# Start of the expert tiles, scaling of their results and the final additions in an attention + mixture-of-experts kernel

## The chip, the cores and the metric

The kernel runs on one core of a Trainium2 chip. The metric is the device time of one execution in microseconds; before the change its median was 694.02 us over three runs (693.63 to 695.32). The engines are TensorE (PE; its weight loads PEld), VectorE (DVE), ScalarE (ACT), GpSimd (POOL) and SyncE (SP), which here only issues transfers.

## The reference, cut to what matters

The input x has 64 batch rows of 128 tokens with 128 features, all fp32. A gated cross-attention with 16 heads (context of 77 tokens) comes first, then a gated mixture of 8 experts:

```python
x = x + tanh(g_xattn[0]) * xattn(layernorm(x), ctx_768, ...)
n = layernorm(x)
gate_scores = softmax(n @ Wg)                       # 8 experts
topk_scores, topk_idx = top_k(gate_scores, 2)
topk_scores = topk_scores / (topk_scores.sum(-1) + 1e-08)
gate  = einsum('bsh,ehi->bsei', n, W11)             # i = 256
value = einsum('bsh,ehi->bsei', n, W12)
fused = gate * sigmoid(gate) * value
expert_out = einsum('bsei,eih->bseh', fused, W2)
x = x + tanh(g_ffn[0]) * sum over the two picked experts of topk_scores * expert_out
```

The kernel computes only the two picked experts of each token: 64 x 128 x 2 = 16,384 token rows.

## The kernel before

**Attention.** The 64 batch rows are handled in 16 groups of 4 (NG, G). A loop over i = 0 to 65 (L970 to L991) does, for one batch row at a time, scores, turning of the probabilities (`turn`) and the product with the values (`mix`, L914). Everything else of a group (loads, layernorm, keys, gate, places, dispatches) is a list of named steps. A planner's table says at which i, and whether before or after the main work of that i (PRE or POST), each step is due (AT, TURN, EARLY, SCHED); `advance(i, where)` runs those that are due. Instructions keep, on each engine, the order in which the program emits them, and each engine works through its own in order.

**From tokens to tiles.** For each group, DVE picks the two experts, POOL counts them (`counts`, L685 to L694), TensorE turns counts into places and DVE into row numbers (`places_in`, `dest` L717). Then POOL writes every token row to its expert's region in DRAM: `dispatch` (L719 to L730) is a memset of a spare buffer of 128x320 (L721), which keeps two indirect transfers apart in time, and an indirect DMA (L722). There are eight to a group, one for each batch row b and choice k (`dispatch{b}{k}`), 128 in all. The groups form two parts: groups 0 to 11 (SPLIT = 12) fill 103 tiles of 128 rows, groups 12 to 15 fill 39. When a part is full, `tiles_count` to `tiles_keep` (L753 to L820) work out which rows and which expert each tile has.

**Tiles.** After the attention loop its pools are closed and those of the tiles are opened in the space that comes free. One step of the tile loop is `tile_steps(t)` (L1081 to L1084), which works on tiles of different age:

- `load` (L1013 to L1021), tile t: SP fetches the tile's rows xt (pool lp, 26 buffers)
- `turned` (L1023), tile t: TensorE transposes (ptt, L1025), DVE copies to xTt (L1027)
- `up` (L1029), tile t-2: two up products pu (L1035), ACT's silu (sgt, L1041), DVE's product (ht, L1043)
- `flip` (L1047), tile t-4: two transposes phh (L1050), ACT's copy to hTt (L1052)
- `down` (L1054), tile t-6: four products pot (L1058), DVE scales by the token's gate weight into y (L1064), then POOL does its memset (L1065) and scatters the rows of y to the result buffer yb in DRAM (L1066)

**Beside the tiles.** The steps of groups 12 to 15 that the attention loop leaves over are in the list `rest` (L1109) and are run a few at each tile, their dispatches included, so POOL does 32 dispatches among its scatters. Results come back by group: `fetch` (L1089, SP) reads both results of each token (ys), `combine` (L1099) adds them to xs with two DVE additions of 128x512 (L1101), `store` (L1103) sends the sum out by ACT's queue. For groups 0 to 11 the table `at` sets the step: fetch of group g at t0 + 2g with t0 = 122, combine three steps and store six steps later. Groups 12 to 15 follow after the tile loop, all fetches first. A fetch waits until all scatters of its part have landed.

Of the kernel before, what the change touches and what calls it, by code (L numbers as in the profile page):

```python
# [8 lines left out]
F32 = mybir.dt.float32  # L9
# [3 lines left out]
AF = mybir.ActivationFunctionType  # L13
ALU = mybir.AluOpType
AX = mybir.AxisListType
PSUM = bass.MemoryType.PSUM
# [5 lines left out]
G = 4  # L22
# [2 lines left out]
JL = 16  # L25
PRE, POST = 0, 1
TOPK = 2
RW = 132
APART = 320
PAST = 1 << 20  # L30
# [2 lines left out]
SPLIT = 12  # L33
# [3 lines left out]
def tile_gated_xattn_moe(  # L37
# [17 lines left out]
    nc = tc.nc  # L55
    B, S, D = x.shape
    M, CD = context.shape[1:]
    E, _, I = W11.shape
    P = 128
    NG = B // G  # L60
# [3 lines left out]
    scale = HD**-0.5  # L64
    NTOK = B * S
    class Part:


        def __init__(self, c, g0, g1):
# [24 lines left out]
    xs = [keep.tile([P, G, D], F32, tag=f"x{g}", name=f"x{g}") for g in range(NG)]  # L94
# [99 lines left out]

    empty = const.tile([P, RW], F32, name="empty")
    nc.gpsimd.memset(empty[:, :D], 0.0)
    nc.gpsimd.iota(empty[:, D:].bitcast(I32), [[0, RW - D]], base=PAST, channel_multiplier=0)
    tg = const.tile([P, 2], F32, name="tg")
# [17 lines left out]
    for q in range(NQ):  # L216
        for k in range(2):
            r = 32 * q + 16 * k
            nc.sync.dma_start(
                out=wo_in[r : r + 16], in_=Wo[32 * q + 16 * (1 - k) : 32 * q + 16 * (2 - k)]  # L220
# [74 lines left out]
    spare_w = const.tile([P, APART], F32, name="spare_w")  # L295
# [12 lines left out]
    with ExitStack() as ph:  # L308
        s2 = ph.enter_context(tc.tile_pool(name="s2", bufs=2))
        s3 = ph.enter_context(tc.tile_pool(name="s3", bufs=3))  # L310
        s4 = ph.enter_context(tc.tile_pool(name="s4", bufs=4))
        s5 = ph.enter_context(tc.tile_pool(name="s5", bufs=5))
        ph.enter_context(tc.manual_schedule(engines={PE, ACT, DVE, POOL}))

        nc.scalar.activation(tg, gates, AF.Tanh)
# [14 lines left out]
        def apart(i, group):  # L330

            i = getattr(i, "ins", i)
            tc.declare_no_dep(i, group=group, reason="rows of their own")
            tc.add_to_no_dep_group(group, i)
# [45 lines left out]
        ring = [ps_r]  # L380
# [4 lines left out]
        def transposed(src, n):  # L385
# [12 lines left out]
        AT = {  # L398
            "loads": (-15, PRE),
            "stats_a0": (-14, PRE),  # L400
            "sel_0": (-14, PRE),
            "stats_a1": (-10, PRE),
            "sel_1": (-13, PRE),
            "shift_a": (-9, POST),
            "sel_2": (-11, POST),
            "context_t": (-7, POST),
# [42 lines left out]
        TURN = {}  # L449
# [157 lines left out]
        def rows_f0(gr, g):  # L607
            pt = part_of(g)
            gr.rows = s5.tile([P, G, TOPK, RW], F32, tag="rows", name=f"rows_{g}")
            gr.xn = gr.rows[:, :, 0, :D]  # L610
            for k in range(TOPK):
                nc.gpsimd.iota(
                    gr.rows[:, :, k, D:].bitcast(I32), [[TOPK, G], [0, RW - D]],
                    base=TOPK * G * (g - pt.g0) + k, channel_multiplier=TOPK * pt.nb,
# [289 lines left out]
        def mix(b, va, pT, gr, n):  # L904
# [23 lines left out]
        NBT = NG * G  # L928
# [16 lines left out]
        EARLY = {  # L945
            (n, 1): 2 * i + where
            for n, i, where in (
                ("rows_a0", 1, PRE), ("rows_a1", 1, PRE), ("context_t", 1, POST),
                ("queries_t", 1, POST), ("queries", 2, POST), ("keys", 2, POST),
            )  # L950
        }
        EARLY["rows_a0", 2], EARLY["rows_a1", 2] = 4, 5
        EARLY["context_t", 2], EARLY["queries_t", 2], EARLY["queries", 2] = 6, 6, 7
        SCHED = {}
        for h in range(2 * min(TURN)[0], 2 * (NBT + 3)):
            for g in range(NG):
                for n in TURN.get((h // 2 - G * g, h % 2), ()):
                    if (n, g) not in FIRST:
                        SCHED.setdefault(EARLY.get((n, g), max(h, 1)), []).append((n, g))

        def run(steps):
            for n, g in steps:
                STEP[n](groups[g], g)

        def advance(i, where):
            run(SCHED.get(2 * i + where, ()))

        pes, vas, pTs = {}, {}, {}
        run(FIRST)
        for i in range(NBT + 2):  # L970
# [10 lines left out]
            if 0 <= i - 2 < NBT:  # L981
                g, b = divmod(i - 2, G)
# [5 lines left out]
                turn_last(pTs[i - 1], i - 1)  # L988
            advance(i, POST)
        advance(NBT + 2, PRE)  # L990
        advance(NBT + 2, POST)  # L991
        at_.close()
        after[0] = True


        lp = ph.enter_context(tc.tile_pool(name="lp", bufs=26))
        yp = ph.enter_context(tc.tile_pool(name="yp", bufs=20))
        hp = ph.enter_context(tc.tile_pool(name="hp", bufs=4))
        cb = ph.enter_context(tc.tile_pool(name="cb", bufs=4))
        ps_u = ph.enter_context(tc.tile_pool(name="ps_u", bufs=2, space=PSUM))  # L1000
        ps_t = ph.enter_context(tc.tile_pool(name="ps_t", bufs=1, space=PSUM))
        ring[0] = ph.enter_context(tc.tile_pool(name="ps_q", bufs=2, space=PSUM))

        wxf = wx.rearrange("p e i -> p (e i)")
        known = "built on the chip from counts, never past the last tile or expert"
# [7 lines left out]
        def load(ti, t):  # L1013
            pt = ti.pt
            r = nc.values_load(
                pt.tab[0:1, 0, ti.k : ti.k + 1], engines=(SP,), min_val=0,
                max_val=E * pt.cap + (pt.spare - 1) * P,
                skip_runtime_bounds_check_because=known,
            )
            ti.x = lp.tile([P, RW], F32, tag="x", name=f"xt_{t}")  # L1020
            nc.sync.dma_start(out=ti.x, in_=pt.xg[bass.ds(r, P), :])  # L1021

        def turned(ti, t):  # L1023
# [28 lines left out]
            nc.scalar.copy(ti.hT, pt)  # L1052

        def down(ti, t):  # L1054
            po = ps_u.tile([P, D], F32, tag="pd", name=f"pot_{t}")
            for c in range(NC):
                w = 2 * I + c * D
                nc.tensor.matmul(  # L1058
                    po, ti.hT[:, c],
                    wxf[:, bass.ds(ti.e + w, D)],  # L1060
                    start=(c == 0), stop=(c == NC - 1),
                )
            y = yp.tile([P, D], F32, tag="y", name=f"y_{t}")
            nc.vector.tensor_scalar_mul(y, po, ti.x[:, D + 1 : D + 2])  # L1064
            nc.gpsimd.memset(spare_w, 0.0)  # L1065
            i = nc.gpsimd.indirect_dma_start(  # L1066
                out=ti.pt.yb[:, :],
                out_offset=bass.IndirectOffsetOnAxis(
                    ap=ti.x[:, D : D + 1].bitcast(I32), axis=0
                ),  # L1070
                in_=y,
                in_offset=None,
                bounds_check=TOPK * ti.pt.ntok - 1,
                oob_is_err=False,
            )
            apart(i, f"results{ti.pt.c}")


        ts = [Tile(pt, k) for pt in parts for k in range(pt.nt)]

        def tile_steps(t):  # L1081
            for lag, f in ((0, load), (0, turned), (2, up), (4, flip), (6, down)):
                if 0 <= t - lag < len(ts):
                    f(ts[t - lag], t - lag)  # L1084


        ys = {}

        def fetch(g):  # L1089
            pt = part_of(g)  # L1090
            ys[g] = cb.tile([P, G, TOPK, D], F32, tag="ys", name=f"ys_{g}")
            i = TOPK * G * (g - pt.g0)
            nc.sync.dma_start(
                out=ys[g].rearrange("p b k d -> p (b k d)"),
                in_=pt.yb.rearrange("(t i) d -> t i d", t=S)[:, i : i + TOPK * G]
                .rearrange("t i d -> t (i d)"),
            )

        def combine(g):  # L1099
            for k in range(TOPK):  # L1100
                nc.vector.tensor_tensor(xs[g], xs[g], ys[g][:, :, k], ALU.add)  # L1101

        def store(g):  # L1103
            nc.scalar.dma_start(
                out=out[G * g : G * g + G].rearrange("b t d -> t b d"), in_=xs[g]
            )


        rest = [  # L1109
            (f, g)  # L1110
            for i in range(NBT + 3, G * (NG - 1) + max(TURN)[0] + 1)
            for where in (PRE, POST)
            for g in range(NG)
            for f in TURN.get((i - G * g, where), ())
        ]
        at = {}
        t0 = parts[0].nt + 19
        for g in range(SPLIT):
            for k, f in enumerate((fetch, combine, store)):
                at.setdefault(t0 + 2 * g + 3 * k, []).append((f, g))  # L1120
        t = 0
        while t < len(ts) + 6 or rest or any(k >= t for k in at):
            tile_steps(t)
# [2 lines left out]
            for f, g in at.get(t, ()):  # L1126
                f(g)
            t += 1
        for g in range(SPLIT, NG):
            fetch(g)  # L1130
        for g in range(SPLIT, NG):
            combine(g)
            store(g)

# [31 lines left out]
```

## Time and profile before

| | us |
|---|---|
| median of three runs | 694.02 |
| the profiled execution, its own time | 692.33 |
| its span on the core | 690.2 |
| PE busy | 615.3 (89%) |
| DVE busy | 466.1 (68%) |
| POOL busy | 442.0 (64%) |
| ACT busy | 392.9 (57%) |

Busy time is an average over stages of different kind: the attention stage runs to about 380 us, the tile stage from there to about 677, and the last four groups' results to 690.2. The profile has a line for each group of instructions (line of the kernel, engine, operation, output<-input and shape, count, busy time, mean of one in ns, and the idle time before it with what ended it). In a timeline a row is a start time, a duration, the engine and the instruction; the brackets at its end hold the engine's idle time before it and what ended that. "issue" is idle time in which the engine waited for nothing that the profile shows.

### The profile page before, as it was taken

The page shows a single profiled execution, that of the slowest core. Times are in us where ns is not written, and L with a number is a line of the kernel's source. Part 1 is how long each engine was busy: PE and PEld are TensorE (multiplying, and loading weights), DVE is VectorE, ACT ScalarE, POOL GpSimd, SP SyncE. Part 2 cuts the span into 40 slices and gives each one's busy share as a digit, 9 for nine tenths or more (in the row PEclk, how much of TensorE's full clock was granted, in tenths as well). Part 3 has the DMA queues.
Part 4 walks back from the last instruction along what each step waited for, and adds up shares of the span by engine and source line. Part 5 has one row for each costly group of instructions (what it writes and reads, how often), then busy time and mean ns, then how long its engine had stood idle before and what let it go on. Part 6 is the DMA issues. An engine that isn't in the chain of part 4 may idle for free.

```text
span 690.2 us, 21369 instructions
## 1 busy us (share of the span) xinstructions
PE 615.3 (89%) x7703; PEld 429.2 (62%) x7703; DVE 466.1 (68%) x1440; ACT 392.9 (57%) x1042; POOL 442.0 (64%) x769
## 2 busy tenths in 40 slices
PE   4799999999999999999988699999978999999770
PEld 3577777776776677676666266666555665656450
DVE  4758798788878887887797356465455454546673
ACT  3697888787877787787655433543432333333220
POOL 4411125577557755765565488888888888887671
PEclk9999999999999999999999899999999999999995
DMA  4493001111110100000110342222222313264666
GB/s 105 124 280 94 16 15 29 38 32 39 33 40 31 32 27 26 26 31 22 34 57 22 84 106 73 75 71 71 80 79 68 103 59 90 80 204 124 194 187 205
DMA packets 64510, 53.55 MB, mean 78 GB/s; under 512 B 14131, under 2 KB 58235, under 8 KB 64408
## 3 DMA queue, kind: packets, MB, share of 16 engines
q1 hardware_dynamic: 46424, 30.52, 16.5%
q0 software_dynamic: 8640, 17.06, 7.5%
q10 hardware_dynamic: 9344, 4.62, 2.4%
q8 instruction: 63, 1.03, 0.6%
q14 instruction: 39, 0.32, 0.2%
HBM read 28.88 MB, written 24.20 MB: 77 GB/s over the span
## 4 chain that ended last, share of the span: by engine, by line
PE 71%; DVE 9%; ACT 6%; issue 5%; POOL 5%; DMA 3%; another core or an unknown queue 1%; POOLq 0%; ACTq 0%; DVEq 0%; SPq 0%
PE pu L1035 16%; PE po L914 11%; PE tp L882 8%; PE pot L1058 7%; PE sc L860 5%; PE phh L1050 4%; PE ptt L1025 3%; PE tl L895 3%; POOL yb L1066 3%; PE pq L561 3%; PE py L584 2%; PE pc L523 2%; PE pg L637 2%; PE pv L833 2%; DVE x L1101 2%
## 5 line engine op out<-in xcount | busy, mean ns | idle before, releaser
L722 POOL DMA_INDIRECT xg<-rows,dest x128 | 127.1, 993 | 66.3 <-DVE gm L644 41.9
L1066 POOL DMA_INDIRECT yb<-y,xt x142 | 140.8, 992 | 41.4 <-issue 13.3
L1035 PE MATMUL pu<-wx,xTt 128*128 x284 | 153.7, 623 | 8.5 <-issue 7.6
L1041 ACT ACTIVATE sgt<-pu 128x256 f32<-128x256 f32 x142 | 54.5, 384 | 170.3 <-PE pu L1035 97.9
L1043 DVE TENSOR_TENSOR ht<-sgt,pu 128x256 f32<-128x256 f32 x142 | 59.6, 420 | 98.9 <-ACT sgt L1041 59.4
L869 DVE TENSOR_REDUCE mx<-sc 128x16 f32<-128x1232 f32 x64 | 91.6, 1431 | 22.4 <-PE sc L860 21.2
L1050 PEld LDWEIGHTS phh<-ident,ht 128*128 128x128 f32 x284 | 39.4, 141 | 79.6 <-issue 68.3
L1058 PE MATMUL pot<-wx,hTt 128*128 x568 | 87.0, 276 | 0.3 <-issue 0.3
L887 ACT ACTIVATE pT<-tp,drop 128x512 f32<-128x512 f32 x128 | 80.3, 677 | 9.9 <-PE tp L882 9.9
L872 DVE TENSOR_TENSOR pe<-sc,mx 128x1024 f32<-128x1024 f32 x64 | 78.4, 1224 | 2.2
L1058 PEld LDWEIGHTS pot<-wx,hTt 128*128 128x128 f32 x568 | 75.0, 192 | 0.4 <-issue 0.4
L914 PE MATMUL po<-pT,own 128*32 128x128 f32 x1536 | 66.9, 274 | 8.1 <-issue 7.8
L882 PEld LDWEIGHTS tp<-ident,pe 128*128 128x128 f32 x512 | 55.6, 142 | 27.9 <-issue 8.9
L882 PE MATMUL tp<-ident,pe 128*128 128x128 f32 x512 | 70.8, 282 | 0.9 <-ACT kb L550 0.6
L914 PE MATMUL po<-pT,va 128*32 128x128 f32 x1536 | 60.8, 274 | 2.3 <-issue 2.0
L1064 DVE TENSOR_SCALAR y<-pot,xt 128x128 f32<-128x128 f32 x142 | 49.0, 347 | 19.9 <-PE ptt L1025 8.5
L1052 ACT COPY hTt<-phh 128x256 f32<-128x256 f32 x142 | 52.3, 368 | 9.8 <-PE ptt L1025 5.5
L1050 PE MATMUL phh<-ident,ht 128*128 128x128 f32 x284 | 54.8, 275 | 3.1 <-ACT hTt L1052 1.9
L914 PEld LDWEIGHTS po<-pT,own 128*32 128x32 f32 x1536 | 46.2, 110 | 17.3 <-issue 17.1
L860 PE MATMUL sc<-kb,qT 32*128 32x308 f32 x512 | 52.5, 480 | 4.4 <-DVE pls L872 2.6
L365 POOL TENSOR_TENSOR rs_a<-rs_a,live 128x4 f32<-128x4 f32 x15 | 3.0, 199 | 81.9 <-ACT rs_a L362 74.1
L1035 PEld LDWEIGHTS pu<-wx,xTt 128*128 128x128 f32 x284 | 43.4, 193 | 19.0 <-issue 17.5
(167 smaller groups left out, 1109.9 us busy)
## 6 DMA issues: line engine op xcount, KB each, us to landing
xt<-xg SPq DMA_DIRECT2D x142, 66.0 KB
ys<-yb SPq DMA_DIRECT2D x16, 512.0 KB
out_dram<-x ACTq DMA_DIRECT2D x16, 256.0 KB
x<-in_x_dram SPq DMA_DIRECT2D x15, 256.0 KB
yb<-y,xt POOLq DMA_INDIRECT x142
wx<-in_L_ffn_W_dram SPq DMA_DIRECT2D x2, 1024.0 KB
xg<-rows,dest POOLq DMA_INDIRECT x128
xg<-empty SPq DMA_DIRECT2D x30, 66.0 KB
```

The lines of the kernel that those rows point to most:

```text
L722: i = nc.gpsimd.indirect_dma_start(out=part_of(g).xg[:, :], out_offset=bass.IndirectOffsetOnAxis(ap=gr.dest[:, k, b : b + 1], axis=0), in_ ...
L860: nc.tensor.matmul(sc[:, q, :W], gr.qT[r, b * S : (b + 1) * S], gr.kb[r, b].rearrange("p h j -> p (h j)"), start=True, stop=True,)
L869: nc.vector.tensor_reduce(mx[:, :, :, 0], sv, AX.X, ALU.max)
L872: nc.vector.tensor_tensor(dst[:, :, :, : j1 - j0], sv[:, :, :, j0:j1], mx.to_broadcast([P, NQ, HQ, j1 - j0]), ALU.subtract,)
L882: nc.tensor.transpose(tp[:, u, :], pe[:, q + u // 2, 2 * (u % 2) : 2 * (u % 2) + 2].rearrange("p h j -> p (h j)"), ident,)
L887: nc.scalar.activation(pT[:, 2 * q : 2 * q + 4], tp, AF.Exp, bias=drop[:, 0, i : i + 1], scale=scale)
L914: nc.tensor.matmul(po[32 * q : 32 * q + 32, v, :], w, pT[:, 2 * q + c if c < 2 else 8 + q // 2, :], start=(c == 0), stop=(c == 2),)
L1035: nc.tensor.matmul(pu.rearrange("p j i -> p (j i)"), ti.xT, wxf[:, bass.ds(ti.e, 2 * I)], start=True, stop=True,)
L1043: nc.vector.tensor_tensor(ti.h.rearrange("p c i -> p (c i)"), sg, pu[:, 1], ALU.mult)
L1050: nc.tensor.transpose(pt[:, c], ti.h[:, c], ident)
L1058: nc.tensor.matmul(po, ti.hT[:, c], wxf[:, bass.ds(ti.e + w, D)], start=(c == 0), stop=(c == NC - 1),)
L1066: i = nc.gpsimd.indirect_dma_start(out=ti.pt.yb[:, :], out_offset=bass.IndirectOffsetOnAxis(ap=ti.x[:, D : D + 1].bitcast(I32), axis=0), i ...
```

## The change

Six edits:

1. A pool l0 with 8 buffers (NL0) is opened beside attention's pools; the rows of the first 8 tiles are loaded into it, the others into lp as before. The pool hp (xT, sg, h, hT) is opened there too. The pools in PSUM are opened in another order, and pot has a pool of its own, ps_d.
2. The dispatches of batch rows 2 and 3 of group 11 are brought forward to the place of 18 after the group's first row, POST. The steps of (NBT + 2, POST), before run ahead of the tiles, become the first of `rest`.
3. y is made by ScalarE (a Copy with the gate weight as its scale) instead of DVE's multiplication.
4. For the last four tiles, POOL's memset covers one column instead of 320.
5. `combine` does one addition. For groups 0 to 11 fetches begin at step 112 (before 122), one each 28/12 steps, and the 24 additions are spread over steps 115 to 141, about one at each; the store goes with the second.
6. Of the last groups, fetched and added in the order 12, 15, 13, 14, group 15's two additions are done by POOL and its store is issued on SP's queue.

```diff
+NL0 = 8
...
+        l0 = ph.enter_context(tc.tile_pool(name="l0", bufs=NL0))
+        hp = ph.enter_context(tc.tile_pool(name="hp", bufs=4))
         ph.enter_context(tc.manual_schedule(engines={PE, ACT, DVE, POOL}))
...
+        for n in ("dispatch20", "dispatch21", "dispatch30", "dispatch31"):
+            EARLY[n, SPLIT - 1] = min(2 * (G * (SPLIT - 1) + 18) + POST, 2 * (G * (SPLIT - 1) + AT[n][0]) + AT[n][1])
...
         advance(NBT + 2, PRE)
-        advance(NBT + 2, POST)
         at_.close()
...
-        hp = ph.enter_context(tc.tile_pool(name="hp", bufs=4))
         cb = ph.enter_context(tc.tile_pool(name="cb", bufs=4))
+        ring[0] = ph.enter_context(tc.tile_pool(name="ps_q", bufs=2, space=PSUM))
+        ps_d = ph.enter_context(tc.tile_pool(name="ps_d", bufs=2, space=PSUM))
+        ps_t = ph.enter_context(tc.tile_pool(name="ps_t", bufs=1, space=PSUM))
         ps_u = ph.enter_context(tc.tile_pool(name="ps_u", bufs=2, space=PSUM))
-        ps_t = ph.enter_context(tc.tile_pool(name="ps_t", bufs=1, space=PSUM))
-        ring[0] = ph.enter_context(tc.tile_pool(name="ps_q", bufs=2, space=PSUM))
...
-            ti.x = lp.tile([P, RW], F32, tag="x", name=f"xt_{t}")
+            ti.x = (l0 if t < NL0 else lp).tile([P, RW], F32, tag="x", name=f"xt_{t}")
...
-            po = ps_u.tile([P, D], F32, tag="pd", name=f"pot_{t}")
+            po = ps_d.tile([P, D], F32, tag="pd", name=f"pot_{t}")
...
-            nc.vector.tensor_scalar_mul(y, po, ti.x[:, D + 1 : D + 2])
-            nc.gpsimd.memset(spare_w, 0.0)
+            nc.scalar.activation(y, po, AF.Copy, scale=ti.x[:, D + 1 : D + 2])
+            nc.gpsimd.memset(spare_w if t < len(ts) - 4 else spare_w[:, 0:1], 0.0)
...
-        def combine(g):
-            for k in range(TOPK):
+        def combine(k):
+            def f(g):
                 nc.vector.tensor_tensor(xs[g], xs[g], ys[g][:, :, k], ALU.add)
...
-            for i in range(NBT + 3, G * (NG - 1) + max(TURN)[0] + 1)
+            for i in range(NBT + 2, G * (NG - 1) + max(TURN)[0] + 1)
...
+            if (i, where) > (NBT + 2, PRE)
...
-        t0 = parts[0].nt + 19
+        t0, n1 = parts[0].nt + 9, 28
         for g in range(SPLIT):
-            for k, f in enumerate((fetch, combine, store)):
-                at.setdefault(t0 + 2 * g + 3 * k, []).append((f, g))
+            for j, f in enumerate((combine(0), combine(1), store)):
+                k = t0 + 3 + (TOPK * g + min(j, 1)) * n1 // (TOPK * SPLIT)
+                at.setdefault(k, []).append((f, g))
+            at.setdefault(t0 + g * n1 // SPLIT, []).append((fetch, g))
...
-        for g in range(SPLIT, NG):
+        last = [(SPLIT, nc.vector), (NG - 1, nc.gpsimd)]
+        last += [(g, nc.vector) for g in range(SPLIT + 1, NG - 1)]
+        for g, _ in last:
             fetch(g)
-        for g in range(SPLIT, NG):
-            combine(g)
-            store(g)
+        for g, on in last:
+            for k in range(TOPK):
+                on.tensor_tensor(xs[g], xs[g], ys[g][:, :, k], ALU.add)
+            store(g, on=nc.sync if on is nc.gpsimd else nc.scalar)
```

More of the change, by code (lines that the diff above doesn't have):

```diff
@@ L1097, in fetch, with store @@
             )
-        def combine(g):
-            for k in range(TOPK):
+        def combine(k):
+            def f(g):
                 nc.vector.tensor_tensor(xs[g], xs[g], ys[g][:, :, k], ALU.add)
-        def store(g):
-            nc.scalar.dma_start(
-                out=out[G * g : G * g + G].rearrange("b t d -> t b d"), in_=xs[g]
+            return f
+        def store(g, b0=0, b1=G, on=nc.scalar):
+            on.dma_start(
+                out=out[G * g + b0 : G * g + b1].rearrange("b t d -> t b d"),
+                in_=xs[g][:, b0:b1],
             )
```

## The prediction, made before the changed kernel was run

> **What bounds the kernel now.** I read the page's slices first, then a table of 50 us windows, then the timelines of the places that the change touches. In the slices, one digit is 17 us:
>
> ```profile
> PE   4799999999999999999988699999978999999770
> POOL 4411125577557755765565488888888888887671
> PEclk9999999999999999999999899999999999999995
> ```
>
> Attention fills the left half and is TensorE's. From slice 24 on (417 us) both PE and POOL look full, so the windows decide (columns: length; busy time and count of PE, PEld, DVE, ACT, POOL; clock; DMA share; GB/s):
>
> ```profile
> 400.00:450.00 50.00, 48.00 (x259) 31.85 (x258) 26.75 (x96) 20.91 (x58) 42.60 (x63) 1.00 0.30 81
> 600.00:650.00 50.00, 44.50 (x218) 27.55 (x216) 28.29 (x84) 16.08 (x48) 38.70 (x57) 1.00 0.53 160
> ```
>
> and POOL's timeline says what its 42.60 of 50 us means:
>
> ```profile
> 560.87 0.97 POOL L1066 DMA_INDIRECT yb<-y,xt  x1 [0.17 <-issue]
> 561.84 0.39 POOL L721 MEMSET spare_w<- 128x320 f32 x1
> 562.39 0.96 POOL L722 DMA_INDIRECT xg<-rows,dest  x1 [0.16 <-issue]
> ```
>
> Every scatter or dispatch is .39 memset + .17 issue + .97 = 1.52 us, and nothing but issue lies between them: POOL is saturated. Following its idle time, it waits for something else than issue only for .53 and 1.77 us around 409 and 417, for 1.77 at 585, and then, from tile 113 (619.3) to tile 136 (667.4), for 11.95 in sum. TensorE's own step is 1.635 us a tile, so PE runs ahead; a scatter starts up to 12 us after its y exists. At tile 113 this lead is used up. What uses it up: 24 of the 142 scalings on DVE (L1064) started over .25 us late, 18.4 us in sum, and 21 of these began just as a POOL memset ended. And then the additions of the late stage:
>
> ```profile
> 646.64 1.41 DVE L1101 TENSOR_TENSOR x<-x,ys 128x512 f32<-128x512 f32 x2
> 647.00 1.16 POOL L1066 DMA_INDIRECT yb<-y,xt  x1 [1.17 <-DVE y L1064]
> 647.97 0.28 DVE L1027 COPY xTt<-ptt 128x128 f32<-128x128 f32 x1
> 649.12 0.97 POOL L1066 DMA_INDIRECT yb<-y,xt  x1 [0.58 <-DVE xTt L1027]
> ```
>
> Both additions run back to back; xTt waits behind them, PE behind xTt, POOL behind y: two tiles take 4.63 us (646.04 to 650.67) where 2 x 1.635 = 3.27 would do. The transition into the tile stage is the other hole:
>
> ```profile
> 375.25 0.97 POOL L722 DMA_INDIRECT xg<-rows,dest  x1 [0.17 <-issue]
> 383.83 1.28 ACT L1041 ACT_TABLE_LOAD   x1
> 384.12 0.45 PE L1025 MATMUL ptt<-ident,xt 128*128 128x128 f32 x1 [4.13 <-DMA xt<-xg]
> 388.96 0.38 ACT L1041 ACTIVATE sgt<-pu 128x256 f32<-128x256 f32 x1 [3.85 <-PE pu L1035]
> ```
>
> The last dispatch of the first part lands at 377.83, but SP's first load starts only at 382.13, since its buffer is attention's and is held for its last readers. PE idles 4.13 us and then runs at clock .50 from 384 to 390. The end:
>
> ```profile
> 675.51 2.11 DMA yb<-y,xt
> 677.68 3.65 DMA ys<-yb
> 681.35 5.52 DVE L1101 TENSOR_TENSOR x<-x,ys 128x512 f32<-128x512 f32 x8 [8.02 <-DMA ys<-yb]
> ```
>
> [...]for the additions: a scatter beside one takes 1.17 instead of .97, the addition stays at .68 to .69. [...]
>
> **The change, part by part**, against the profiled span of 690.2.
>
> *Early loads.* Eight tiles get buffers beside attention, and the instruction order shows that their loads wait for DMA queues alone. The dispatches of rows 2 and 3 of group 11 move ahead of group 12's counts on POOL, into its idle 5.39 us at 364 to 370, so all dispatches of part 0 can land by about 371 and the loads, .83 us apart, by 378. ptt_0 can follow PE's last mix at once[...]. Not all of it counts: ACT's table for L1041 is loaded only after its attention work, at 385.1. Before, the third up product starts at 391.57; after, I put it at 385.1 + .38 (sg_0) + .42 (h_0) and one tile more, 386.8. That is **-4.7**, between -3 and -6. Four dispatches are moved past counts on POOL's queue; the work in that gap hides them. If it does not (4 x 1.52 = 6.1), group 12's counts come late, which delays only part 1, long before it is due. The (NBT+2, POST) steps go among the tiles: same instructions, in engines with idle time there.
>
> *POOL's early wait* of .53 at 409 is TensorE's ramp: **-0.5**.
>
> *y on ScalarE.* 142 instructions leave DVE (.347 each) and join ACT. ACT's price: [...]ACT's 128x128 copies out of PSUM without a pointer take 270 to 290 here, its 128x256 ones with a pointer 481, so .36 to .39, and I take .39. ACT's step is then .38 (sg) + .37 (hT) + .39 = 1.14 of 1.635: the cover is its idle time, and this costs **0** on the path. Without cover it would cost .39 a tile. DVE's step becomes .28 + .42 = .70, or 1.39 with one addition. The late y vanish with their place on DVE; while POOL is the bound, that only adds to PE's lead.
>
> *Additions one at a time.* 24 of .69, one to a step from step 115 instead of pairs from 125. DVE needs 1.39 of 1.635, so no step grows. I count POOL saturated to its last scatter: of the 11.95 of waits after 619, I take 1.5 as left, since ys_0 can only be fetched after the 103rd scatter, and the addition at step 115 waits for it with DVE's xTt and h, and so PE, behind it; POOL then lives on its queue of about 2.5 tiles[...]. **-10.5** (-12 to -5).
>
> *Contention.* 24 separate additions can each meet a scatter, against 11 meetings before: 13 x .2 = +2.6 at worst; below nothing is excluded, as a scatter cannot be quicker than .97. About 5 more: **+1.0**.
>
> *Last four memsets* one column wide: POOL's 128x256 memset takes .301 and the 128x320 one .387, which runs to nothing at one column; its shortest additions (128x8) take .20. So 4 x .19 to .39, and I take **-1.0**.
>
> *Tail.* DVE does 6 x .69 = 4.14 instead of 5.52, GpSimd two additions of 512 columns. Their price: POOL's 77x308 product takes .836 us, 2.7 ns a column, so 1.4 each[...]. Beside DVE, that is -1.4. But [...]taking turns they need 4.14 + 2.8 = 6.9, +1.4. I take **0**, both ends in the range.
>
> Sum: -4.7 - 0.5 - 10.5 + 1.0 - 1.0 + 0 = **-15.7**. The span becomes 674.5, with the 2.1 us around it (692.33 - 690.2) 676.6. The median before, 694.02, is 1.0024 times the profiled time, so the forecast is **678.3**.
>
> **The rivals.**
> A, the forecast: POOL is the bound to the end, 678.3; own range 673 to 683 from the ends above. For it: nothing but issue between POOL's instructions for 170 us.
> B, the chain PE, ACT, DVE starves POOL in the last 30 tiles: y, now in ACT's queue behind hT and sg, or a DVE addition ahead of xTt lengthens each of 33 steps (115 to 147) by .2: +6.6, about **684.5**. For it: PE already takes 1.635 and the cover on POOL is 2.5 tiles. Against: DVE and ACT both have slack. A variant in which the early loads are held after all, so that the change doesn't do what it says there, loses the 4.7 and gives 683.0.
> C, more is gained: start -6, tail -1.4, and the waits of 1.77 at 417 and 585, for which no late y accounts, vanish as well: 678.3 - 1.3 - 1.4 - 3.5 = **672.1**.
> D, slower: the fetches, ten steps earlier, come while results and loads use the same DMA engines; each group's first addition then waits for its transfer at the head of DVE's queue, with xTt behind it[...]. To undo 15.7 us over 12 groups it must hold DVE 1.3 us a group once POOL's queue is empty; at 1.5 it is +18, **697**. For it: a fetch took 3.65 us at the end. Against: three steps, 4.9 us, lie between fetch and addition, and DMA was busy .30 to .53.
>
> **How the numbers follow.** A .62, B .20, C .13, D .04, and .01 for losses that happen to cancel the gain. Predicted is A. The range runs from just under C to just over B, 671.5 to 686. Faster by over 0.3% (about what a measurement of this kernel can tell from no change): A, B and C, .95; same .01; slower .04.
>
> **What would show it.** Right: the first transpose within 1 us of the last mix, with no .50 clock; the third up product near 387; y on ACT at .39 and no cluster of late y; POOL's waits other than issue after tile 113 under 2 us; last scatter near 660; additions apart on DVE, xTt on time. Wrong: POOL waiting "<-ACT y" in the last thirty tiles (B), a first load still behind attention (B's variant), DVE's additions waiting for ys at every group (D). A POOL step other than 1.52 would upset everything, since 1.52 carries the forecast.

## The result, and the profile after

The changed kernel takes 683.1 us (median of four, 682.56 to 686.94) against 693.83 for the kernel before, run beside it; the ratio is .9854, with an interval of .9826 to .9882. The forecast was 678.3, so the change went the way that was foreseen, by two thirds of the size. Of the six runs of one kernel below (one column in every memset) two were in a slower state; its time, 731.9, is the median of the other four (735.88 over all six). The profiled execution took 683.43 us, its span 681.7 (690.2 before).

The slices of the page, for the same three rows as before:

```profile
PE   4799999999999999999988799989988989999980
POOL 4411125667576757664647477888888888788782
PEclk9999999999999999999999899999988999999995
```

The dent at the transition is smaller, and the late part of PE is fuller. In the windows (length; PE, PEld, DVE, ACT, POOL; clock; DMA share; GB/s) PE gains 4 us in the late stretch. DVE's load has gone over to ACT; in the late stretch DVE stays as busy as before (29.54, 28.29 before), since 20 of the additions now fall into it instead of 10:

```profile
400.00:450.00 50.00, 48.48 (x270) 32.81 (x269) 21.54 (x72) 31.50 (x88) 42.98 (x65) 1.00 0.27 75
600.00:650.00 50.00, 48.53 (x248) 30.89 (x247) 29.54 (x75) 27.05 (x84) 40.75 (x60) 1.00 0.76 228
```

Five marks divide each profiled execution into pieces that add up to its span. "Again" is a second profile of the changed kernel:

| | before | after | again |
|---|---|---|---|
| attention's last product ends | 379.99 | 381.52 | 379.57 |
| third up product starts | 391.57 | 389.05 | 386.10 |
| first scatter starts | 396.85 | 395.50 | 392.33 |
| 114th scatter (tile 113) starts | 619.29 | 618.13 | 615.62 |
| last scatter (tile 141) starts | 675.51 | 665.58 | 663.11 |
| from the last scatter to the end | 14.7 | 16.1 | 15.8 |

The first scatter (of a tile's results by POOL) gained 1.35 us in the one profile and 4.5 in the other. The stretch from tile 113 to 141 fell from 56.2 to 47.5 in both. The tail grew by 1.1 to 1.4. Between the first scatter and tile 113 nothing was won (222.4 before; 222.6 and 223.3).

**The transition after.** The timeline, with the rows that matter here ("remote" stands where the view finds no instruction that has just ended and could be the releaser):

```profile
381.45 0.33 PE L1033 MATMUL ptt<-ident,xt 128*128 128x128 f32 x1
382.19 0.98 POOL L727 DMA_INDIRECT xg<-rows,dest  x1 [0.17 <-issue]
383.16 0.38 POOL L726 MEMSET spare_w<- 128x320 f32 x1
383.57 0.27 ACT L926 COPY os<-po 128x128 f32<-128x128 f32 x1 [1.53 <-remote]
383.60 0.29 DVE L1035 COPY xTt<-ptt 128x128 f32<-128x128 f32 x1 [1.37 <-remote]
383.95 0.33 PE L1033 MATMUL ptt<-ident,xt 128*128 128x128 f32 x1 [2.17 <-DVE xTt L1035]
```

The first transpose now follows the last product at once: the early loads do what they should. But its result, ready at 381.8, is taken up by DVE at 383.60 only, and ACT takes up attention's last product just as late, at 383.57. Both begin as a memset of POOL ends (383.16 + .38 = 383.54). TensorE waits 2.17 us for DVE, and its clock falls again, for a shorter time than before the change (at .50 for 3.4 us, before for 6.8):

```profile
384.00:386.00 2.00, 1.25 (x3) 0.72 (x4) 0.85 (x2) 1.98 (x6) 1.81 (x5) 0.75 0.42 102
386.00:388.00 2.00, 2.00 (x4) 0.73 (x3) 0.50 (x3) 1.09 (x2) 1.79 (x3) 0.50 0.41 99
388.00:390.00 2.00, 2.00 (x5) 0.58 (x4) 1.09 (x7) 0.38 (x1) 0.00 (x0) 0.89 0.51 98
```

In the second profile TensorE waits about as long there (2.12 us), yet its clock stays at 1.00, and the first scatter comes 12.8 us after attention's last product instead of 14.0.

The trace also keeps the times at which an engine's semaphore was raised, that is, at which its signal "finished" went out. The two products of TensorE that ended at 381.52 and 381.78 have theirs at 383.54 and 383.58; ACT and DVE start .02 us after them. So the takers did not dawdle: the signals came late. TensorE itself did not stand still either, as a later place shows, where the transpose had ended at 488.82:

```profile
488.99 1.12 PE L1043 MATMUL pu<-wx,xTt 128*128 x2 [0.17 <-issue]
490.47 0.29 DVE L1035 COPY xTt<-ptt 128x128 f32<-128x128 f32 x1 [1.42 <-PE phh L1058]
```

TensorE began its next products while DVE waited for the signal of the transpose. (The view names phh, the last to end before the copy's start; the copy needs the transpose alone.)

**The late stage after.** One step out of it, to be set beside 646 to 649 us of the kernel before:

```profile
638.82 0.38 ACT L1072 ACTIVATE y<-pot,xt 128x128 f32<-128x128 f32 x1
639.04 0.68 DVE L1110 TENSOR_TENSOR x<-x,ys 128x512 f32<-128x512 f32 x1
639.48 1.09 POOL L1075 DMA_INDIRECT yb<-y,xt  x1 [0.53 <-ACT y L1072]
639.64 0.28 DVE L1035 COPY xTt<-ptt 128x128 f32<-128x128 f32 x1
```

xTt now waits for one addition instead of two; in this stage it starts .66 us after its transpose on the mean. POOL still waits for y, .53 us here. Its waits from 612 us on, first of the kernel before, then of the changed one (sum, times, longest):

```profile
POOL yb L1066 <- DVE y L1064: 8.7, 10, 1.2
POOL yb L1066 <- DVE xTt L1027: 6.3, 13, 0.7
```

```profile
POOL yb L1075 <- ACT y L1072: 7.3, 17, 0.9
POOL yb L1075 <- issue: 2.1, 12, 0.2
```

The .17 of issue in each taken off, POOL's waits after 600 us went from 11.95 to 5.3 us (5.95 in the second profile), not to 1.5. The step in this stage is 1.77 us (from the scatter of tile 114, 619.76, to that of tile 137, 660.48), .13 over TensorE's own 1.635 and .25 over POOL's 1.52: over 23 tiles that .25 makes the waits. No signal for xTt or y is over .25 us late after 613 us in either profile, so what lengthens the step here is the addition ahead of xTt.

**The tail after:**

```profile
671.56 1.42 DVE L1152 TENSOR_TENSOR x<-x,ys 128x512 f32<-128x512 f32 x2 [11.86 <-DMA ys<-yb]
672.83 2.61 POOL L1152 TENSOR_TENSOR x<-x,ys 128x512 f32<-128x512 f32 x2 [6.27 <-DMA ys<-yb]
674.46 3.58 DVE L1152 TENSOR_TENSOR x<-x,ys 128x512 f32<-128x512 f32 x4 [1.48 <-DMA ys<-yb]
```

GpSimd's two additions take 1.27 us each and lie beside DVE's work. But DVE stands still for 1.48 us until its next 512 KB has landed: the transfers land 1.3 to 1.6 us apart (by the starts of the additions that wait for them), and DVE needs only 1.4 for a group. And its next four additions take 3.58 us instead of the 2.75 that four take elsewhere: the first of them, begun at 674.46 beside GpSimd's second, lasts 1.52 us.

### The profile page after: what moved, and what is told of

Its sections match the earlier page's. It is cut to its first block, busy times and chain, and to the rows that moved or that the text cites. A ratio compares the mean times of both kernels' runs of the same rounds, so it can differ in the third digit from the quotient of the medians.

```text
span 681.7 us, 21362 instructions
## 1 busy us (share of the span) xinstructions
PE 615.6 (90%) x7703; PEld 429.9 (63%) x7703; DVE 431.0 (63%) x1296; ACT 441.6 (65%) x1184; POOL 443.1 (65%) x771
## 3 DMA queue, kind: packets, MB, share of 16 engines
q8 instruction: 63, 1.03, 0.7%
## 4 chain that ended last, share of the span: by engine, by line
PE 80%; ACT 6%; DVE 6%; issue 5%; DMA 2%; POOL 1%; another core or an unknown queue 0%; SPq 0%; ACTq 0%; DVEq 0%; POOLq 0%
PE pu L1043 20%; PE po L919 12%; PE pot L1066 9%; PE tp L887 8%; PE sc L865 6%; PE phh L1058 5%; PE ptt L1033 3%; PE tl L900 3%; PE pq L566 2%; PE py L589 2%; PE pg L642 2%; PE pv L838 2%; PE pc L528 2%; ACT pT L892 1%; PE pk L549 1%
## 5 line engine op out<-in xcount | busy, mean ns | idle before, releaser
L1075 POOL DMA_INDIRECT yb<-y,xt x142 | 139.7, 984 | 34.8 <-issue 15.9
L1051 DVE TENSOR_TENSOR ht<-sgt,pu 128x256 f32<-128x256 f32 x142 | 59.8, 421 | 112.0 <-issue 53.2
L874 DVE TENSOR_REDUCE mx<-sc 128x16 f32<-128x1232 f32 x64 | 91.6, 1431 | 24.4 <-PE sc L865 19.3
L1072 ACT ACTIVATE y<-pot,xt 128x128 f32<-128x128 f32 x142 | 52.5, 369 | 28.4 <-PE ptt L1033 12.8
L1035 DVE COPY xTt<-ptt 128x128 f32<-128x128 f32 x142 | 40.9, 288 | 39.5 <-PE ptt L1033 14.9
```

The costliest lines, as they stand in the source:

```text
L874: nc.vector.tensor_reduce(mx[:, :, :, 0], sv, AX.X, ALU.max)
L1051: nc.vector.tensor_tensor(ti.h.rearrange("p c i -> p (c i)"), sg, pu[:, 1], ALU.mult)
L1075: i = nc.gpsimd.indirect_dma_start(out=ti.pt.yb[:, :], out_offset=bass.IndirectOffsetOnAxis(ap=ti.x[:, D : D + 1].bitcast(I32), axis=0), i ...
```

## The experiments

Each was timed beside the kernel before, on the same chip. The first two sets ran on one chip (kernel before: 694.13 and 692.98 us). The third set ran on another one, where the kernel before takes 656.03 us; ratios of that set are not compared with those of the first two.

### First set: parts of the change undone

**No early dispatches** (changed kernel, the two lines of `EARLY` taken out):

```diff
-        for n in ("dispatch20", "dispatch21", "dispatch30", "dispatch31"):
-            EARLY[n, SPLIT - 1] = min(2 * (G * (SPLIT - 1) + 18) + POST, ...
```

> The changed kernel without the forward move of group 11's dispatches. In the changed kernel attention's last product ends at 381.52 instead of 379.99, and the first scatter came only 1.35 us earlier than before the change, not 4.7. Theory 1: the move itself delays attention through POOL's queue; without it the last product ends near 380.0, the first scatter comes near 394 and the time falls by about 1.4 us. Theory 2: the delay arises at 341 to 343 us, ahead of every moved instruction, where a DVE reduction began 1.5 us after TensorE had finished its input; it is an accident of phase, so the last product stays near 381.5 (380 to 382), the loads begin 2 to 3 us later than the 375.8 of the changed kernel, and the time stays within 1 us of it.

684.64 us, ratio .9869 (.9848 to .9889). Attention's last product ends at 379.78, but the next three kernels keep the early dispatches and have it at 379.97, 379.31 and 378.66. So the later end in the profile after was an accident of that execution, as theory 2 has it, although this kernel's own end also fits theory 1. The first loads go out at 377.85, and still ahead of the first transpose. That is 5.5 us later than the 372.39 of the profile after (the 375.8 of the expectation was its fifth load). The medians differ by 1.5 to 1.8 us and the intervals overlap, so what the move is worth was not settled.

**y on DVE again:**

```diff
-            nc.scalar.activation(y, po, AF.Copy, scale=ti.x[:, D + 1 : D + 2])
+            nc.vector.tensor_scalar_mul(y, po, ti.x[:, D + 1 : D + 2])
```

> The changed kernel with y scaled by DVE again. Theory 1 (the prediction's): ScalarE's part costs nothing and mainly empties DVE; on DVE a step with an addition then takes .28 + .42 + .35 + .69 = 1.74, over TensorE's 1.635, so the 26 steps from the 115th scatter on grow by .1 to .2 each: +3 to +5 us, all after 618 us. Theory 2: the late stage is set by end signals of TensorE that reach the other engines late, whichever engine scales: within 1 us of the changed kernel.

687.13 us, ratio .990 (.988 to .992), 4 us above the changed kernel. The stretch from tile 113 to 141 takes 50.2 us instead of 47.5. Theory 1 holds: the move matters where an addition shares DVE's step.

**Additions in pairs:**

```diff
-                k = t0 + 3 + (TOPK * g + min(j, 1)) * n1 // (TOPK * SPLIT)
+                k = t0 + 3 + TOPK * g * n1 // (TOPK * SPLIT)
```

> The changed kernel with both additions of a group at the step of the first one. Theory 1: taking the additions apart is what shortened the stretch from the 113th scatter to the last, from 56.2 to 47.5 us; in pairs DVE holds up xTt and then TensorE again by about .5 to .7 us a group: +5 to +8 us. Theory 2: y's move to ScalarE did it, since DVE's two steps with a pair are 2 x .70 + 1.38 = 2.78 of 3.27: within 1.5 us of the changed kernel.

688.43 us, ratio .9934 (.9909 to .9959), 5 us above the changed kernel; the stretch takes 53.2 us, and POOL's waits after 600 us are 11.0, close to the kernel before. Theory 1 holds. The two edits add up: 47.5 + 2.7 + 5.7 = 55.9, and 56.9 with the 1.0 of the last four memsets, where the kernel before, with none of them, has 56.2.

**Tail on DVE alone**, in the order 12, 13, 14, 15:

```diff
-        last = [(SPLIT, nc.vector), (NG - 1, nc.gpsimd)]
-        last += [(g, nc.vector) for g in range(SPLIT + 1, NG - 1)]
+        last = [(g, nc.vector) for g in range(SPLIT, NG)]
```

> The changed kernel with the last four groups in the order 12, 13, 14, 15, all additions on DVE and all stores on ScalarE's queue. In the changed kernel it takes 16.1 us from the last scatter's start to the end, before the change 14.7. Theory 1: GpSimd's two additions (2.61 us beside DVE's) and SP's store cost that: 14.7 again, -1.4 us. Theory 2: the four 512 KB transfers set it, DVE follows them: 16.1 stays, within .5 us.

680.05 us (678.35 to 680.65), ratio .9796 (.9777 to .9815): faster than both kernels. Yet from the last scatter to the end it takes 15.6 us, against 16.1 and 15.8 of the changed kernel, so in these profiles the tail gave .2 to .5 us of the 3 by which this kernel is faster; theory 2 is nearer for the tail itself. All profiles together say a little more: the seven tails with GpSimd take 15.8 to 16.5 us, the six with DVE alone 14.6 to 15.6, on the mean .9 less. DVE waits there too, .83 us for the second transfer, while no addition is lengthened (six in 4.08 us). The rest of the gain lies in the tile stage (tile 113 to 141 in 45.2 us, waits of 1.7), whose instructions are the same, in the same order on every computing engine. It entered this stage with a lead: y of tile 113 was ready 1.9 us before its scatter, against .3 in both profiles of the changed kernel. Where that lead came from is open.

### Second set: a control, and parts of the change alone

> The changed kernel once more, as a control. In the kernels run so far whose attention is instruction for instruction the same, its last product ended at 381.5, 380.0, 379.3 and 378.7 us, and POOL's waits after 600 us differed by 3.6 us between two kernels with the same tile stage. Theory 1: this is phase, which changes from one execution to the next: the time lies between 680 and 684, the last product ends anywhere from 378.6 to 381.6. Theory 2: the last groups' order and engine are worth 3 us: 683 to 684 again, with POOL's waits after 600 near 5 us.

682.80 us (680.56 to 685.78), ratio .9859 (.9829 to .9889). Attention's end at 379.57 confirms that it varies by itself from one execution to the next, and so theory 1 for the start. POOL's waits after 600 us are 5.95 again, which speaks for theory 2 on the late stage: the kernel with the tail on DVE is better there by more than chance between two executions.

**Additions apart, alone** (kernel before, with `combine(k)`, t0 = 112, n1 = 28 of the change):

```diff
-        t0 = parts[0].nt + 19
+        t0, n1 = parts[0].nt + 9, 28
...
+            for j, f in enumerate((combine(0), combine(1), store)):
```

> The kernel before with one edit: additions one at a time, with the new steps of fetches and stores; y stays on DVE. Theory 1: taking apart works only with DVE emptied, since .28 + .42 + .35 + .69 = 1.74 is over TensorE's 1.635: the stretch from the 113th scatter to the last goes from 56.2 to 51 to 53, the time to 689 to 691. Theory 2: taking apart is the whole of the late gain: 47 to 49 us for the stretch, 685 to 687.

689.08 us, ratio .9942 (.9925 to .996). The stretch takes 50.6 us: theory 1. With y on DVE the work of DVE in a step with an addition is .1 over TensorE's 1.635, with y on ACT it is under it. TensorE's step from tile 114 to 137 was 1.89 here and 1.76 in the changed kernel.

**The start alone** (kernel before, with l0, hp, the PSUM pools, the early dispatches and the longer `rest`):

```diff
+            ti.x = (l0 if t < NL0 else lp).tile([P, RW], F32, tag="x", name=f"xt_{t}")
...
-        advance(NBT + 2, POST)
```

> The kernel before with the edits at the start alone: rows of the first eight tiles in places of their own, four dispatches earlier, the steps after attention among the tiles, PSUM pools in the new order. From the five profiled kernels with these edits the first scatter comes 13.9 to 14.8 us after attention's last product, before the change 16.9. Theory 1: POOL carries this to the end: -2 to -3 us, 691 to 692. Theory 2: the additions in pairs at the end give it back: within 1 us of before.

690.85 us, ratio .9955 (.9936 to .9974). The first scatter comes 14.7 us after attention's last product (16.9 before). Theory 1: this gain lasts to the end. The parts now make the whole: 1 - .9955 = .45% from the start, .58% from additions apart, and .43% from y on ACT (.990 to about .9857) make 1.46%; measured were 1.46 and 1.41%. Each part has an interval of about .2% to either side, and memsets and tail are not in the sum, so that the agreement is closer than the measurements can bear out.

**One column in every memset** (changed kernel):

```diff
-                nc.gpsimd.memset(spare_w, 0.0)
+                nc.gpsimd.memset(spare_w[:, 0:1], 0.0)
...
-            nc.gpsimd.memset(spare_w if t < len(ts) - 4 else spare_w[:, 0:1], 0.0)
+            nc.gpsimd.memset(spare_w[:, 0:1], 0.0)
```

> The changed kernel with one column instead of 320 in every memset ahead of a dispatch or a scatter. POOL's step becomes about 1.28 instead of 1.52. Theory 1: POOL is the bound from 417 to 618 us and signals are late because POOL is always at work; with it faster, TensorE's 1.635 us a tile is left: the last scatter at about 394 + 15 + 126 x 1.64 to 1.75, 616 to 630, the time 632 to 646. Theory 2: TensorE's steps are held up for other reasons (its pace was 2.0 us a tile from 575 to 618, with scatters ready to go): the pace stays, the time falls by less than 12 us.

731.9 us, ratio 1.0559 (1.0501 to 1.0618): 49 us slower than the changed kernel. Neither theory foresaw that. Its timeline at the transition:

```profile
407.95 0.33 PE L1033 MATMUL ptt<-ident,xt 128*128 128x128 f32 x1
409.40 0.11 POOL L726 MEMSET spare_w<- 128x1 f32 x1
409.71 0.97 POOL L727 DMA_INDIRECT xg<-rows,dest  x1 [0.19 <-issue]
411.17 0.98 POOL L727 DMA_INDIRECT xg<-rows,dest  x1 [0.16 <-issue]
412.46 0.96 POOL L727 DMA_INDIRECT xg<-rows,dest  x1 [0.19 <-issue]
412.86 0.29 DVE L1035 COPY xTt<-ptt 128x128 f32<-128x128 f32 x1 [4.12 <-remote]
```

A copy that needs nothing but the transpose starts 4.6 us after that has ended by the profile's model, having sat through several POOL transfers. Attention ends at 408.0 instead of 379.6, so its own dispatches seem to do the same to it. DVE's waits there say for whom:

```profile
DVE mx L874 <- PE sc L865: 40.3, 22, 7.6
```

In the changed kernel this line has 19.3 us in 18 waits with a longest of 3.5. Hence a third theory: on this chip DVE and ACT learn late that TensorE has finished, while POOL issues indirect transfers close upon each other; the memset of .39 us is the pause in which they learn it. With the pause of .12 they learn it after two, three or more transfers. That fits the starts at the ends of memsets: of the late starts of xTt and y (by over .25 us) 45 of 71 in the profile after lie within .1 us of one, but 2 of 45 here. It is TensorE's signals that are late. DVE's ht, which waits for ACT in nearly every tile, never starts over .03 us after ACT has finished and DVE is free, in this kernel too. That POOL's transfers are what holds the signals is argued from these times; no run on this chip took the transfers away. What holds them inside the chip, no view shows.

### Third set, on the other chip

**No scatters on POOL** (changed kernel, memset and scatter replaced by a plain transfer of y):

```diff
-            i = nc.gpsimd.indirect_dma_start(
...
+            i = nc.scalar.dma_start(out=ti.pt.yb[r0 : r0 + P, :], in_=y)
```

> The changed kernel in which POOL scatters nothing: memset and scatter of the 142 tiles are left out, and y goes as a plain block of 128 rows to the result buffer by ScalarE's queue, so that the rows land in other places than they should. Theory 1: POOL's indirect transfers, one after the other, are what keeps TensorE's end signals from DVE and ScalarE, and POOL is the bound: with POOL idle from the last dispatch on, fewer than 5 of the copies xTt and of the y start over .25 us late, TensorE runs at 1.635 us a tile, the last y comes near 394 + 141 x 1.64 = 625, the time is near 645. Theory 2: the lateness is TensorE's own: 20 to 35 late ones of each kind as in the changed kernel, pace 2.0 us around tile 105, the time above 660.

638.29 us, ratio .9729 (.9693 to .9766). No xTt and two y start over .25 us late. By itself this would be theory 1, but in the other three kernels of this set, in which POOL scatters as ever, no xTt and no y is late either: on this chip the lateness does not arise, and the run can't tell why it arises on the first. What it does show is the pace that is left without POOL's scatters: from the first y to the last it takes 251.8 us, 1.79 a tile. From tile 80 to 103, ahead of the additions, TensorE's step is 1.635; from tile 112 to 127, with an addition at most steps, 1.80. So the additions lengthen TensorE's step on this chip too, with no xTt late.

**Group 12's dispatches later** (changed kernel):

```diff
+        QUIET = [(f"dispatch{b}{k}", SPLIT) for b in range(G) for k in range(TOPK)]
...
+        rest = [s for s in rest if s not in QUIET]
+        rest[16:16] = QUIET
```

> The changed kernel with group 12's eight dispatches moved from the transition to behind the eleventh scatter. Theory 1: at the transition it is these dispatches, back to back, that kept TensorE's first end signals from DVE (xTt of tile 0 started 1.4 us after its transpose) and so halved TensorE's clock again: now xTt starts within .4 us, the clock stays over .9, the first scatter comes 11 to 12.5 us after attention's last product instead of 13.9 to 14.8; what POOL does not do there it does later, 5 x 1.52 = 7.6 us, so the time rises by 3 to 6 us. Theory 2: the signal is late by itself (a long queue on TensorE): xTt starts over 1 us late again, the first scatter does not move.

667.85 us, ratio 1.0177 (1.0147 to 1.0208). The first copy starts .4 us after its transpose's end, but so it does in the next two kernels, with POOL at work, so the run is no test of the signals. The first scatter comes 14.5 us after attention's last product, against 11.4 and 11.5 in those two: DVE's steps for the gate come between the first and second xTt, TensorE waits 1.93 us, and the clock is .50 at 362 to 366. From the 13th to the 91st scatter it takes 170.1 us instead of some 160 (160.1 on the first chip, and half way between the two kernels below). So moving eight dispatches, 8 x 1.52 = 12 us, out of POOL's idle time costs nearly all of that where POOL is the bound.

**A shorter and a longer memset** (kernel with the tail on DVE):

```diff
-APART = 320
+APART = 256
```

> The kernel with the tail on DVE (680.05), its spacing memset 256 columns instead of 320, .30 instead of .39 us. Theory 1: the memset is the pause in which the other engines' waiting signals pass; with one column the kernel took 736, so a shorter pause costs more than POOL gains: 685 to 700. Theory 2: POOL's 1.52 is the bound and becomes 1.43: 142 + 32 steps less the share that isn't bound, 110 x .09 = 10: 668 to 672.

> The same kernel with a memset of 384 columns, about .47 us. Theory 1: POOL's step becomes 1.60, still under TensorE's 1.635 once the dispatches are over, so only the 417 to 585 us stretch grows, 110 x .08 = 9, and fewer late signals at the end give back 0 to 4: 684 to 690. Theory 2: what is lost to late signals weighs more than POOL's own time: 676 to 680.

649.53 us, ratio .9889 (.9857 to .9921), with 256 columns; 660.74, ratio 1.007 (1.0045 to 1.0095), with 384. The memset of a tile takes .333 and .441 us in them, .385 with 320. From the 13th to the 91st scatter, a stretch with 102 memsets, it takes 154.7 and 165.4 us. The memsets in it take 34.2 and 45.0 us: of 10.9 us more work on POOL, 10.7 are found in the time. POOL is the bound there. So a shorter memset makes the kernel faster, as theory 2 has it for 256 columns, and a longer one slower, as theory 1 has it for 384. The sizes can't be compared, since both expectations start from the first chip's 680, and the kernel with 320 columns was not run here. Half the difference between the two times is 5.6 us, where I had expected 10 and 9. The timeline of the kernel with 384 columns shows the transition as the prediction had imagined it:

```profile
358.30 0.33 PE L1033 MATMUL ptt<-ident,xt 128*128 128x128 f32 x1
358.81 0.25 ACT L926 COPY os<-po 128x128 f32<-128x128 f32 x1
359.01 0.28 DVE L1035 COPY xTt<-ptt 128x128 f32<-128x128 f32 x1
359.10 0.98 POOL L727 DMA_INDIRECT xg<-rows,dest  x1 [0.17 <-issue]
359.35 0.33 PE L1033 MATMUL ptt<-ident,xt 128*128 128x128 f32 x1 [0.73 <-DVE xTt L1035]
```

POOL is no less busy than on the first chip (5.38 of the six us from 358; 5.27 of the six from 382 in the profile after), and the copy comes within .4 us. Its waits hold one more thing, the addition at the head of DVE's queue that waits for the first fetch:

```profile
DVE x L1110 <- DMA ys<-yb: 9.5, 1, 9.5
```

PE's lead over POOL, 14.6 us at tile 104, is 1.9 at tile 112 after that, and POOL hardly notices. This is the wait that the prediction named at step 115. In the two profiles of the changed kernel on the first chip it does not arise: the lead at tile 104 is 2.5 and .9 us, and no wait of DVE's L1110 for ys is in the profile. The kernel with y on DVE, with a lead of 8.1 there, has one of 1.2 us.

The kernel of the mean of 256 and 384 columns, which is that with 320, would take about 655 on this chip: an estimate, half way between the two times. It is within 1 us of the kernel before. The changed kernel itself was not run there, so whether the change gains anything on that chip is open.

## Why the prediction was right, and where it was off

The direction and the cause of the largest gain were right: POOL is the bound until its supplier's lead is used up, and additions that hold up xTt and y cost it time at the end. The gain was 4.8 us smaller than forecast. The 683.1 lies inside the stated range of 671.5 to 686, but nearer to rival B (684.5) than to A (678.3), and just outside A's own 673 to 683; so the width of the range made it right, not A's sum. By the ends that the prediction gives for each part, A's range would have been 672.5 to 688.7. (B's own sum is 684.9, and D's 696.3.) Of the signs of being right, the first transpose at the last mix, the early third up product and the price of y came true; the late y, POOL's waits and the last scatter (665.6 and 663.1, not 660) did not, and of the signs of being wrong B's came: POOL waits "<-ACT y".

By its own steps, with the mean of the two profiles:

**Early loads, -4.7 and -0.5.** Right for the loads, mis-sized for what follows. The first scatter gained 1.35 and 4.5, on the mean 2.9. Attention's end, which varies by itself from 378.7 to 381.8 in six profiles of kernels with the same early edits on that chip, is no part of the change. From attention's last product to the third up product it fell from 11.6 us to 7.5 and 6.5, as much as was foreseen, although the wait of 2.1 us for the late signal, which the prediction did not have, stood in it (5.2 us on the second chip, without that wait). From there to the first scatter it grew from 5.3 to 6.5 and 6.2: the steps of (NBT + 2, POST), costed at nothing, now stand between the first tiles' copies on DVE, from 389.7 to 390.6 in the profile after. That is 1.1 us of the difference; no run took these steps out again. The separate gain of .5 did not come: from the first scatter to the 13th it takes 25.2 us before and 25.3 after.

**y on ScalarE, 0.** Its price was right (.369 us measured, .36 to .39 foreseen). Taken out alone it costs 4 us, since DVE's step with an addition is then over TensorE's; the prediction had this within the -10.5. Its reading of the late y was wrong, though. They were to vanish "with their place on DVE"; in the profile after 35 y on ACT and 36 xTt start over .25 us late (24 and 9 before), in sum 54 us. So what lies behind the 21 coincidences with POOL's memset is not DVE's alone: y on ACT is late more often. The signal from TensorE was late, for ACT as well: for the two products that ended at 381.52 and 381.78 it went out 2.0 and 1.8 us after the end. The move even brought more of it: in the five profiles of the first chip with y on ACT and the memset of .39 us, 24 to 35 y and 26 to 36 xTt are late, in the four with y on DVE 10 to 24 and 8 to 15. Why is open. With that, PE's lead did not grow: at tile 104 it was 2.5 and .9 us, against 5.0 before and 8.1 with y on DVE again, and at tile 113 it was used up as before.

**Additions apart, -10.5.** This is the term that failed in size: waits fell by 6.0 to 6.6. 5.3 to 5.95 us stayed, not 1.5. The step that failed is "so no step grows". DVE's 1.39 us of work do fit into TensorE's 1.635, but an addition can stand ahead of xTt, and TensorE's step grew to 1.76. Without a lead POOL then waits for the difference to its 1.52 at each tile. The kernel with all of the tail on DVE, which had 1.9 us of lead at tile 113, waited only 1.7 us in sum. So rival B had the mechanism: POOL did wait "<-ACT y" in the last thirty tiles, since "a DVE addition ahead of xTt" lengthened the steps, by .13 instead of the .2 that B names. ACT's queue had no part in it: y starts .08 us after its product on the mean.

**Contention, +1.0.** Wrong in sign. The sum of the scatters' durations fell from 140.8 to 139.7 us. Single additions still lengthen scatters that they meet (1.03 to 1.09), but for less than .2.

**Last four memsets, -1.0.** Right: .12 instead of .39, four times, is 1.08.

**Tail, 0.** +1.3 in the two profiles, near the upper end (+1.4), but not for its reason: that all additions of the two engines take turns was an estimate, and one of DVE's was lengthened. Begun beside GpSimd's second, it took 1.52 us instead of .69, .83 more. The transfers set the pace, so a second adder had little to win. Over all profiles GpSimd's part costs the tail .9 us. Why it takes 15.6 with all additions on DVE, and 14.7 before, is not settled.

The sum of these terms: 2.9 + 8.75 - 1.3, less .5 lost between the first scatter and tile 113, is 9.9 us of span, and the mean of the two spans, 680.3, lies 9.9 below 690.2, as it must: the five pieces make up the span.

## What to carry to other kernels

If an engine is the bound, work out what becomes of its supplier's lead: a gain upstream shows only at the place where that lead runs out. When one engine's instructions start late at the ends of another's, look whether a third engine shows it too before naming a shared resource. And a pause that looks like waste on the bounding engine may be what lets the others go on: change its length in small steps, and on more than one chip.

## What the runs showed of the hardware that I had not expected

- Two chips of the same kind run the kernel before in 693 and 656 us. The instructions last the same (scatter .99, mx 1.43 us on both). On the first, 36 xTt and 35 y started over .25 us late in the profile after, and of two of TensorE's products among POOL's indirect transfers the signals went out 2.0 and 1.8 us after the ends; in the four profiles of the second, no xTt is late.
- On the first chip the length of the pause between two such transfers matters: with .39 us the copies xTt came up to 1.9 us late, with .12 us up to 4.1, and the kernel became 7% slower than the changed one while POOL's own work became 73 us shorter (443.1 to 369.8).
- An addition of 128x512 takes 1.27 us on GpSimd and .69 on DVE; where one of DVE's began beside GpSimd's, it took 1.52 in the profile after and 1.3 to 1.8 in five others.
- A wait of TensorE of 2.1 to 2.2 us, followed by little work, came before a clock of .50 in one profile of the changed kernel (386 to 388 us) and before one of 1.00 in the other.
